# VectorE's reads of projections, bias products, norm roots and score tests issued one to three steps later

## Chip, core and metric

The kernel runs on one core of a Trainium2 chip, as one program. The metric is the device time of that core in microseconds (us), over all of its work from the inputs in HBM to the output in HBM. The core has five engines that run side by side, each in the order of its own queue: TensorE (PE; its weight loads are PEld), VectorE (DVE), ScalarE (ACT), GpSimd (POOL) and SyncE (SP), which here issues nearly all DMAs.

## What is computed

Four images of 32 x 32 positions with 256 channels pass through four layers. Layer 0 and the first part of layer 3 are state-space blocks with a scan over the 1024 positions; layer 1 is a grouped-convolution bottleneck; layer 2 is a masked attention and a mixture of eight experts; layer 3 ends with another mixture. Cut to what matters here, with the bookkeeping between the layers left out:

```python
# layer 0, one image; layer 3's scan is alike with 16 states instead of 64
x = conv3x3(layernorm(src) @ w_in)             # 512 channels, depthwise
x = gelu(x)
dt = softplus(dt_raw @ w_dt + dt_bias)          # dt_raw, Bm, Cm = split(x @ w_x)
def step(h, inp):
    xt, dtt, Bt, Ct = inp
    h = exp(dtt[:, :, None] * A) * h + (dtt * xt)[:, :, None] * Bt[:, None, :]
    return h, einsum('bdn,bn->bd', h, Ct)
out = src + layernorm(scan(step) + x * D_skip) @ w_out
# layer 1: relu(x + conv1x1(relu(conv3x3_grouped(relu(conv1x1(x))))))
# layer 2: y = layernorm(x + softmax(QK/sqrt(32) + mask) V Wo); then
#          y + sum over the best two of eight experts (gelu(y @ w1) @ w2)
# layer 3: scan block (gated by silu), then a second mixture of experts
```

## The kernel before, in words

**Scans.** The function `scans` (line 384) runs eight passes in the order of `SCANS` (line 32): (0,0), (0,1), (3,0), (0,2), (3,1), (0,3), (3,2), (3,3), where (0,b) is layer 0's scan of image b and (3,b) layer 3's. A pass of layer 0 has 256 units and one of layer 3 has 64, 1280 units together. A unit holds 128 pairs of channel and state on the partitions and all 1024 positions along the row. For each unit SyncE loads dt rows (dA), ScalarE makes the decay by an exponential, TensorE spreads the input of 32 channels over the partitions (`first`, tile ps_rep, bf16, two buffers of PSUM), VectorE multiplies by the B rows (TENSOR_TENSOR on ps_rep) and runs the scan instruction (TENSOR_TENSOR_SCAN, tile h), GpSimd multiplies h by the C rows, and for every two units TensorE collects the states (`pair`, tile ps_y). `scans` is a generator: it yields twice a unit, after the product and after the scan, so a unit has two half steps. Ahead of the last pass stand four empty units (`DRAIN`).

**Stages.** Everything else is written as twelve stages (`STAGES`, line 34), generators that yield after each small step: `front` makes layer 0's scan inputs of an image, `middle` takes the finished scan of layer 0 through `back0`, `layer1`, `attention`, `moe` and `front3`, which makes layer 3's scan inputs, and `last` takes layer 3's scan through `back3` and the second `moe` to the output. For image 3, `middle` is interleaved with `back3` and `moe` of image 2 (`beside`).

**What sets the order.** `run` (line 620) goes through the half steps of `scans` and after each draws up to two steps (`TICKS`) of the current stage by `advance`. It stops drawing in a half step when an engine's planned time has come ahead of VectorE's (`LEAD`), by fixed costs that the class `Metered` (line 99) adds up; these costs decide the order of instructions alone. `need` (line 583) is the one exception: when a pass is about to begin and its inputs are not yet made, it draws steps of the stage without any scan between them until they are. At the first pass, that is at the start, and at the last pass, (3,3), it has to.

**The reads.** `pipe` (line 200) runs a list of items through a list of functions, the second function one tick behind the first, the third two ticks behind, and yields once a tick. The usual first function is a product on TensorE into PSUM, and the second VectorE's read of it: in `back0` `turn` and `stats` (transposition and statistics), `project` and `add`; in `layer1` `up` and `add`; in `moe` `last` and `add` (the product of routing weights and biases, tile ps_b); in `back3` `project` and `add` (tile ps_o). `rstd` (line 254) computes 1/sqrt(v) for a normalisation: ScalarE takes Ln and Exp, then VectorE refines by one Newton step, four operations on `_w` and `_r` tiles straight behind; it is called by `norm` (tiles ln_, lnm_, lnt_, lny_) and by `back0` (b_). `large_scores` (line 1374) tests whether the scores of attention can grow large: squares on ScalarE, two products into ps_n, maxima on VectorE (top), a transposition by TensorE, and the comparison on VectorE (most, large), on which all engines then branch (line 1319). PSUM for the stages has three buffers that `ps` (line 194) hands out in turn.

Of the kernel before, what the change touches and what calls it, by code (L numbers as in the profile page):

```python
# [12 lines left out]
ALU = mybir.AluOpType  # L13
AX = mybir.AxisListType
# [6 lines left out]
TB = L // P  # L21
# [28 lines left out]
LEAD, LAG, TICKS = 0.0, 4.0, 2  # L50
# [89 lines left out]
END = object()  # L140


class Hybrid:
    def __init__(self, ctx, tc, a, out):
        self.ctx, self.tc, self.nc, self.a = ctx, tc, tc.nc, a
# [54 lines left out]
    def pipe(self, items, *steps, cost=1.0, cut=False):  # L200


        items = list(items)
        for tick in range(len(items) + len(steps) - 1):
            for s in reversed(range(len(steps))):
                if 0 <= tick - s < len(items):
                    steps[s](items[tick - s])
                    if cut and s:
                        yield cost
            yield cost if tick < len(items) else 0.5  # L210
# [43 lines left out]
    def rstd(self, pool, var, eps, n, tag):  # L254


        nc = self.nc
        v = pool.tile([P, n], F32, tag=tag + "_v", name=tag + "_v")
        nc.vector.tensor_scalar(v, var, eps, None, ALU.add)
        r = pool.tile([P, n], F32, tag=tag + "_r", name=tag + "_r")  # L260
        self.log_table()
        nc.scalar.activation(r, v, AF.Ln)
        nc.scalar.activation(r, r, AF.Exp, scale=-0.5)
        w = pool.tile([P, n], F32, tag=tag + "_w", name=tag + "_w")
        nc.vector.tensor_tensor(w, r, r, ALU.mult)
        nc.vector.tensor_tensor(w, w, v, ALU.mult)
        nc.vector.tensor_scalar(w, w, -0.5, 1.5, ALU.mult, ALU.add)
        nc.vector.tensor_tensor(r, r, w, ALU.mult)
        return r
# [4 lines left out]
    def norm(self, pool, src, n, out, tag):  # L274

        nc = self.nc
        mv = pool.tile([P, n, 2], F32, tag=tag + "_mv", name=tag + "_mv")

        def stats(j):
            st = pool.tile([P, 6], F32, tag=tag + "_st", name=tag + "_st", bufs=2)  # L280
            nc.vector.bn_stats(st, src[:, j, :])
            nc.vector.bn_aggr(mv[:, j, :], st)

        yield from self.pipe(range(n), stats, cost=0.8)
        r = self.rstd(pool, mv[:, :, 1], 1e-5, n, tag)
        yield 0.8
        b = pool.tile([P, n], F32, tag=tag + "_b", name=tag + "_b")
        nc.vector.scalar_tensor_tensor(b, mv[:, :, 0], -1.0, r, ALU.mult, ALU.mult)
        yield 0.5
        for j in range(n):  # L290
            nc.scalar.activation(
                out[:, j, :], src[:, j, :], AF.Identity, bias=b[:, j : j + 1], scale=r[:, j : j + 1]
            )
            if j % 4 == 3:
                yield 0.7
# [324 lines left out]
    def run(self):  # L620

        self.done, self.ready = set(), set()
        self.todo, self.stage, self.wait = list(STAGES), None, None
        self.alone, self.reached, self.passed = False, 0, set()
        nc, tc = self.nc, self.tc
        with tc.tile_pool(name="scan", bufs=1) as mp, tc.tile_pool(
            name="scps", bufs=1, space=PSUM
        ) as psum, tc.tile_pool(name="sdps", bufs=1, space=PSUM) as side, tc.manual_schedule():
            self.side_psum(side)
            self.scan_psum = psum  # L630
            self.mask_work, self.sorted = self.setup(), False
            clock = self.clock = dict.fromkeys(Metered.COST, 0.0)
            self.nc = Metered(nc, clock)
            for n, _ in enumerate(self.scans(mp, psum)):
                now = clock["vector"]
                if n % 2 and clock["gpsimd"] < now:
                    next(self.mask_work, None)
                for e in clock:
                    clock[e] = max(clock[e], now - LAG)
                for _ in range(TICKS):  # L640
                    if max(clock.values()) > clock["vector"] + LEAD or self.advance() is None:
                        break
            while self.advance() is not None:
                pass
            self.nc = nc
        assert not self.todo
# [275 lines left out]
    def back0(self, b, tb):  # L922


        nc, tc, vec = self.nc, self.tc, self.vec
        with tc.tile_pool(name=f"k{b}", bufs=1, side="right") as sp:
            nc.sync.dma_start(tb, self.image(self.a["x"].rearrange("b h w c -> (b h w) c"), b))
            y = sp.tile([P, DC, L], F32, name="y_back")
            u = sp.tile([P, DC, L], F32, name="u_back")
            w_out = sp.tile([P, DC, C], F32, name="w_out0")  # L930

            def fetch(d):
                nc.sync.dma_start(u[:, d, :], self.mem["u", 0, b, d])
                yield from self.scanned((0, b), [y[:, k, :] for k in range(DC)], d)

            def skip(d):
                nc.vector.scalar_tensor_tensor(
                    y[:, d, :], u[:, d, :], vec["L0_conv_D_skip"][:, d : d + 1], y[:, d, :],
                    ALU.mult, ALU.add,
                )  # L940

            yield 1.0
            yield from fetch(0)
            yield from self.add_rows(tb, self.bout0, TB)
            nc.sync.dma_start(w_out, self.mem[("w_out0",)])
            for d in range(1, DC):
                yield from fetch(d)
                for _ in range(4):
                    yield 0.5
                skip(d - 1)  # L950
                yield 1.3
            for _ in range(4):
                yield 0.5
            skip(DC - 1)
            yield 1.3
            mv = sp.tile([P, TB, 2], F32, name="b0mv")
            got = {}

            def turn(j):
                got[j] = ps = self.ps("ps_yt")  # L960
                for d in range(DC):
                    nc.tensor.transpose(
                        ps[:, d * P : (d + 1) * P], y[:, d, j * P : (j + 1) * P], self.ident
                    )

            def stats(j):
                st = sp.tile([P, 6], F32, tag="b0st", name="b0st", bufs=2)
                nc.vector.bn_stats(st, got.pop(j))
                nc.vector.bn_aggr(mv[:, j, :], st)

            yield from self.pipe(range(TB), turn, stats, cost=1.0)
            r = self.rstd(sp, mv[:, :, 1], 1e-5, TB, "b0")
            yield 0.8

            def project(j):
                got[j] = ps = self.ps("ps_o")
                for d in range(DC):
                    nc.tensor.matmul(
                        ps[:, :C], lhsT=y[:, d, j * P : (j + 1) * P], rhs=w_out[:, d, :],
                        start=(d == 0), stop=(d == DC - 1),  # L980
                    )

            def add(j):
                nc.vector.scalar_tensor_tensor(
                    tb[:, j, :], got.pop(j)[:, :C], r[:, j : j + 1], tb[:, j, :], ALU.mult, ALU.add
                )

            yield from self.pipe(range(TB), project, add, cost=1.7)

# [40 lines left out]
    def layer1(self, b, tb):  # L1032
        nc, tc = self.nc, self.tc
        with tc.tile_pool(name=f"l1{b}", bufs=1, side="right") as fp:
# [56 lines left out]
                nc.vector.tensor_tensor(tj, got.pop(j), tj, ALU.add)  # L1091
                nc.scalar.activation(tj, tj, AF.Relu)

            yield from self.pipe(range(TB // 2), up, add, cost=1.0)

# [276 lines left out]
    def large_scores(self, fp, qT, kT, large):  # L1374


        nc = self.nc
        sq = fp.tile([P, 2, 2, L], F32, name="sq")
        top = fp.tile([P, 2], F32, name="top2")
        for i, x in enumerate((qT, kT)):  # L1380
            for c in range(2):
                nc.scalar.activation(sq[:, i, c, :], x[:, c, :], AF.Square)
                yield 0.8
        for g in range(2):
            n2 = self.ps("ps_n2")
            for r in range(4):
# [2 lines left out]
                    rhs=sq[:, r // 2, r % 2, g * 512 : (g + 1) * 512],  # L1389
                    start=True, stop=True, tile_position=(0, 32 * r),  # L1390
                )
            nc.vector.tensor_reduce(top[:, g : g + 1], n2, AX.X, ALU.max)
            yield 1.3
        nc.vector.tensor_tensor(top[:, 0:1], top[:, 0:1], top[:, 1:2], ALU.max)
        ps = self.ps("ps_n3", (P, 2, 64))
        nc.tensor.transpose(ps[:1].rearrange("o i r -> o (i r)"), top[:, 0:1], self.ident)
        most = fp.tile([1, 2], F32, name="most")
        nc.vector.tensor_reduce(most, ps[:1], AX.X, ALU.max)
        nc.vector.tensor_tensor(most[:, 0:1], most[:, 0:1], most[:, 1:2], ALU.mult)
# [211 lines left out]
    def moe(self, which, b, tb, side="right", pause=False):  # L1611

        nc, tc, a = self.nc, self.tc, self.a
# [6 lines left out]
        with ExitStack() as stack:  # L1620
# [22 lines left out]
            with tc.tile_pool(name=f"mg{which}{b}", bufs=1, side=side) as gp:  # L1643
# [52 lines left out]
                    tj = tb[:, 2 * j : 2 * j + 2, :]  # L1696
                    nc.vector.tensor_tensor(tj, got.pop(j), tj, ALU.add)

                yield from self.pipe(range(TB // 2), last, add, cost=1.0)

            if pause:
                yield END
# [230 lines left out]
    def back3(self, b, tb, side="right", pause=False):  # L1933
        nc, tc = self.nc, self.tc
        with tc.tile_pool(name=f"h{b}", bufs=1, side=side) as sp:
# [68 lines left out]
                        add(j)  # L2004
                        yield 0.5
            else:
                yield from self.pipe(range(TB // 2), project, add, cost=3.4)

    def until(self, *what):
        while what not in self.passed:  # L2010
# [157 lines left out]
```

## Time and profile before

| | |
|---|---|
| median of 3 runs | 6303.35 us (6299.39 to 6311.23) |
| the profiled execution | 6294.21 us |
| its span, first to last instruction | 6292.5 us |
| mean granted TensorE clock | 0.842 |
| scan instruction (DVE, 128x1024) | 1280 times, 2285 ns, 2924.3 us |
| product ahead of it (DVE, ps_rep) | 1280 times, 1210 ns, 1549.4 us |
| product behind it (POOL, h) | 1280 times, 2366 ns, 3024.2 us |
| ACT, decay (two passes' kinds) | 1024 + 256 times, 1142 and 1143 ns |
| moved by DMA | 934.97 MB, 149 GB/s on the mean |

How to read it: times in a timeline are microseconds from the first instruction of the span. A row of groups has the line, the engine, the operation, the tiles out<-in, the shape and the count, then busy time and mean duration in ns, then idle time ahead of it and what ended that. Line 131 is the helper through which all recorded operations pass, so the tile's name tells the operation. A row of waits reads: engine and tile, what it waited for, microseconds in total, how often, and the longest. In rows by stretch, each engine's busy microseconds are followed by the number of its instructions; behind them stand the granted TensorE clock, the share of DMA engines busy, and GB/s.

### The profile page before, as it was taken

Reading aid. Unit: us, or ns where it says so; the run is one execution under the profiler, and the core shown is the slowest. Engines: PE = TensorE matmul, PEld = TensorE weight load, DVE = VectorE, ACT = ScalarE, POOL = GpSimd, SP = SyncE. Lnnn points to the kernel's source line nnn. Section 1 sums busy time; section 2 is a strip of 40 time slices with the busy share of each in tenths; the row PEclk is TensorE's granted clock in tenths of the full one; section 3 lists DMA queues with packets and bytes.
Section 4 is the critical chain, followed back from the end, with each engine's and each line's share of the span. In section 5 each row is a group of like instructions: output and inputs, shape, how many; then the busy total and the mean of one; then the engine's idle time right before and its main releaser. Section 6 shows DMA issues by size and latency. Waiting matters only on the chain. (4 is left out here: it accounts for less than half of the span.)

```text
span 6292.5 us, 59823 instructions
## 1 busy us (share of the span) xinstructions
PE 5142.7 (82%) x20249; PEld 2117.1 (34%) x20249; DVE 5032.7 (80%) x4016; ACT 3410.6 (54%) x4299; POOL 3825.9 (61%) x1948
## 2 busy tenths in 40 slices
PE   5676785579798568979869969989689779997999
PEld 2122120132253122234225522244145332543566
DVE  5888898988898998889889988899889982317811
ACT  3565655345496435558638735567547544336621
POOL 2787768665586766568767756577867752006600
PEclk7687785589798668979969979979779889999989
DMA  3555555544355656445455576345545761027611
GB/s 109 160 158 167 165 175 185 159 150 136 113 173 177 194 165 170 132 128 191 159 178 174 182 179 165 119 150 195 174 156 179 208 161 48 19 73 184 166 34 34
DMA packets 347915, 934.97 MB, mean 149 GB/s; under 512 B 37748, under 2 KB 120256, under 8 KB 345984
## 3 DMA queue, kind: packets, MB, share of 16 engines
q1 hardware_dynamic: 344880, 928.38, 48.7%
q0 software_dynamic: 2128, 2.13, 0.2%
q8 instruction: 165, 2.70, 0.2%
q14 instruction: 166, 1.36, 0.1%
q10 hardware_dynamic: 576, 0.39, 0.0%
HBM read 841.02 MB, written 92.37 MB: 148 GB/s over the span
## 5 line engine op out<-in xcount | busy, mean ns | idle before, releaser
L131 POOL TENSOR_TENSOR h<-h,rows 128x1024 f32<-128x1024 f32 x1280 | 3024.2, 2366 | 1740.4 <-DVE h L131 1529.3
L131 DVE TENSOR_TENSOR_SCAN h<-dA,ps_rep 128x1024 f32<-128x1024 f32 x1280 | 2924.3, 2285 | 182.2 <-ACT dA L131 53.6
L131 DVE TENSOR_TENSOR ps_rep<-ps_rep,rows 128x1024 f32<-128x1024 f32 x1280 | 1549.4, 1210 | 142.6 <-PE ps_rep L131 141.7
L131 PE MATMUL ps_rep<-S,spread_L_conv_A_log 96*128 96x512 bf16 x2048 | 752.8, 456 | 770.3 <-DVE h L131 722.4
L131 ACT ACTIVATE dA<-dA,A_L_conv_A_log 128x1024 f32<-128x1024 f32 x1024 | 1125.4, 1142 | 440.0 <-DMA dA<-dt 405.7
L131 PE MATMUL ps_y<-h,collect_L_conv_A_log 128*32 128x512 f32 x4096 | 704.4, 741 | 15.3 <-POOL h L131 15.3
L131 PE MATMUL ps_e<-we,h_m 128*128 128x256 f32 x3072 | 709.4, 383 | 8.3 <-ACT h_m L131 8.3
L131 PEld LDWEIGHTS <-spread_L_conv_A_log 96*128 96x128 bf16 x2048 | 159.7, 102 | 1558.0 <-DVE h L131 1246.4
L131 PEld LDWEIGHTS ps_e<-we,h_m 128*128 128x128 f32 x3072 | 583.3, 191 | 159.2 <-ACT h_m L131 31.0
L131 PE MATMUL ps_h<-xTm,we 128*128 128x512 f32 x1280 | 603.3, 607 | 4.6 <-DMA we<-in_L_ffn_W_dram 4.5
L131 ACT ACT_TABLE_LOAD x402 | 515.8, 1283 | 37.0 <-PE ps_h L131 15.5
L131 ACT ACTIVATE h_m<-ps_h,cols 128x512 f32<-128x512 f32 x384 | 257.5, 686 | 423.0 <-PE ps_h L131 421.0
L131 ACT ACTIVATE p<-ps_sc 128x512 f32<-128x512 f32 x404 | 219.3, 594 | 316.7 <-PE ps_sc L131 306.1
L131 ACT ACTIVATE dA<-dA,A_L_attn_A_log 128x1024 f32<-128x1024 f32 x256 | 282.8, 1143 | 141.4 <-DMA dA<-dt 122.8
L131 PEld LDWEIGHTS ps_h<-xTm,we 128*128 128x128 f32 x1280 | 242.2, 193 | 281.0 <-issue 211.5
L131 PE MATMUL ps_rep<-S,spread_L_attn_A_log 96*128 96x512 bf16 x512 | 176.8, 433 | 160.2 <-DVE h L131 138.6
L131 PE MATMUL ps_at<-p,v 128*32 128x512 f32 x1024 | 270.7, 608 | 0.2 <-ACT p L131 0.2
L131 PE MATMUL ps_at<-p,ones 128*32 128x512 f32 x1024 | 270.7, 608 | 0.0
L131 DVE SCALAR_TENSOR_TENSOR tb_rows<-ps_e,cw,tb_rows 128x256 f32<-128x256 f32 x128 | 55.7, 477 | 242.8 <-PE ps_e L131 242.7
L131 PE MATMUL ps_sc<-qT,kT 32*128 32x512 f32 x808 | 244.0, 654 | 4.6 <-ACT p L131 2.0
L131 PE MATMUL ps_cv<-pad,diag 128*128 128x512 f32 x504 | 230.5, 597 | 0.0
L131 PEld LDWEIGHTS ps_y<-h,collect_L_conv_A_log 128*32 128x32 f32 x4096 | 93.2, 118 | 339.7 <-issue 216.6
(347 smaller groups left out, 5475.6 us busy)
## 6 DMA issues: line engine op xcount, KB each, us to landing
dA<-dt SPq DMA_DIRECT2D x1280, 512.0 KB
we<-in_L_ffn_W_dram SPq DMA_DIRECT2D x64, 512.0 KB
parts<-parts SPq DMA_DIRECT2D x60, 384.0 KB
S<-parts SPq DMA_DIRECT2D x90, 256.0 KB
dt<-sp_r SPq DMA_DIRECT2D x64, 256.0 KB
y<-yo SPq DMA_DIRECT2D x128, 128.0 KB
y_back<-y SPq DMA_DIRECT2D x64, 256.0 KB
we<-in_L_ffn_w_dram SPq DMA_DIRECT2D x64, 256.0 KB
```

The costliest lines, as they stand in the source:

```text
L131: return got(*args, **kw)
```

## The change

A class `Slot` marks a yielded step that ends the half step's drawing: when `run` draws a `Slot`, it goes on to the next half step of the scans. `pipe` takes None as a function that does nothing, so that `pipe(items, product, None, read)` puts the read two ticks behind the product instead of one. This is done at five places (back0 twice, layer1, moe's bias product, back3 where it is not run beside another stage). `rstd` becomes a generator that yields three Slots between ScalarE's Exp and VectorE's refinement. `large_scores` issues both products, a Slot after each and one more, then both maxima, and another Slot behind the transposition. Nothing that is computed changes.

```diff
+class Slot(float):
+    pass
...
-                if 0 <= tick - s < len(items):
+                if steps[s] and 0 <= tick - s < len(items):
                     steps[s](items[tick - s])
...
         nc.scalar.activation(r, r, AF.Exp, scale=-0.5)
+        for _ in range(3):
+            yield Slot(0.5)
         w = pool.tile([P, n], F32, tag=tag + "_w", name=tag + "_w")
...
                 for _ in range(TICKS):
-                    if max(clock.values()) > clock["vector"] + LEAD or self.advance() is None:
+                    if max(clock.values()) > clock["vector"] + LEAD:
+                        break
+                    cost = self.advance()
+                    if cost is None or isinstance(cost, Slot):
                         break
...
-            yield from self.pipe(range(TB), turn, stats, cost=1.0)
-            r = self.rstd(sp, mv[:, :, 1], 1e-5, TB, "b0")
+            yield from self.pipe(range(TB), turn, None, stats, cost=1.0)
+            r = yield from self.rstd(sp, mv[:, :, 1], 1e-5, TB, "b0")
...
-            yield from self.pipe(range(TB), project, add, cost=1.7)
+            yield from self.pipe(range(TB), project, None, add, cost=1.7)
...
-            yield from self.pipe(range(TB // 2), up, add, cost=1.0)
+            yield from self.pipe(range(TB // 2), up, None, add, cost=1.0)
...
+        sums = []
         for g in range(2):
             n2 = self.ps("ps_n2")
...
-            nc.vector.tensor_reduce(top[:, g : g + 1], n2, AX.X, ALU.max)
-            yield 1.3
+            sums.append(n2)
+            yield Slot(1.3)
+        yield Slot(0.5)
+        for g in range(2):
+            nc.vector.tensor_reduce(top[:, g : g + 1], sums[g], AX.X, ALU.max)
         nc.vector.tensor_tensor(top[:, 0:1], top[:, 0:1], top[:, 1:2], ALU.max)
         ps = self.ps("ps_n3", (P, 2, 64))
         nc.tensor.transpose(ps[:1].rearrange("o i r -> o (i r)"), top[:, 0:1], self.ident)
+        yield Slot(0.5)
...
-                yield from self.pipe(range(TB // 2), last, add, cost=1.0)
+                yield from self.pipe(range(TB // 2), last, None, add, cost=1.0)
...
-                yield from self.pipe(range(TB // 2), project, add, cost=3.4)
+                yield from self.pipe(range(TB // 2), project, None, add, cost=3.4)
```

More of the change, by code (lines that the diff above doesn't have):

```diff
@@ L284, in norm @@
         yield from self.pipe(range(n), stats, cost=0.8)
-        r = self.rstd(pool, mv[:, :, 1], 1e-5, n, tag)
+        r = yield from self.rstd(pool, mv[:, :, 1], 1e-5, n, tag)
         yield 0.8
```

## Prediction

> **What bounds the kernel now.** I read the page's busy shares first, then VectorE's waits up to the last scan of the seventh pass, then the busy time by stretch, and last the two places that decide this change. VectorE is the busiest engine over most of the span:
>
> ```profile
> PE 5142.7 (82%) x20249; PEld 2117.1 (34%) x20249; DVE 5032.7 (80%) x4016; ACT 3410.6 (54%) x4299; POOL 3825.9 (61%) x1948
> ```
>
> Four stretches of busy time (PE, PEld, DVE, ACT, POOL, then the granted clock):
>
> ```profile
> 0.00:5230.10 5230.10, 4160.31 (x16443) 1579.30 (x16444) 4646.28 (x3467) 2989.55 (x3769) 3593.16 (x1819) 0.82 0.53 162
> 5230.10:5679.30 449.20, 418.33 (x1739) 194.54 (x1739) 90.30 (x233) 163.23 (x226) 37.27 (x29) 0.94 0.16 47
> 5679.30:5957.10 277.80, 250.14 (x958) 130.09 (x957) 244.44 (x184) 194.40 (x210) 188.11 (x95) 0.96 0.73 186
> 5957.10:6292.50 335.40, 313.93 (x1114) 213.17 (x1112) 51.63 (x133) 63.45 (x96) 7.31 (x5) 0.94 0.12 37
> ```
>
> The first is seven of the eight passes of scans (1216 of 1280), bound by VectorE at 89%. The second has no scan at all: the last pass needs what the stage of image 3 makes, the stage is not done, and TensorE works alone (93%). I call it the gap. The third is the last pass, the fourth the tail. VectorE's timeline shows the gap's two ends, and TensorE's (third line) where attention of image 3 ends:
>
> ```profile
> 5227.82 2.29 DVE L131 TENSOR_TENSOR_SCAN h<-dA,ps_rep 128x1024 f32<-128x1024 f32 x1 [0.39 <-ACT dA L131]
> 5679.32 1.23 DVE L131 TENSOR_TENSOR ps_rep<-ps_rep,rows 128x1024 f32<-128x1024 f32 x1 [4.55 <-PE ps_rep L131]
> 5396.85 3.29 PE L131 MATMUL ps_wo<-w_L_attn_Wo,raw 128*128 128x256 f32 x14 [1.93 <-POOL raw L131]
> ```
>
> So the time is the sum of the scans' stretch and the gap, then two stretches that the change hardly touches. VectorE's waits at the sites it moves, within the first stretch:
>
> ```profile
> DVE lny_w L131 <- ACT lny_r L131: 22.5, 6, 7.0
> DVE tb L131 <- PE ps_o L131: 21.2, 8, 6.0
> DVE tb L131 <- PE ps_b L131: 14.5, 7, 2.1
> DVE top L131 <- PE ps_n L131: 12.1, 8, 2.9
> ```
>
> With norm roots ln, lnm, b0, lnt (3.2+2.8+2.3+2.1), most (1.6) and b0's statistics (0.6) they make 82.9 us, the ceiling of the gain. 4.0 of it (top 3.0, most 0.5, lnt 0.5) belongs to image 3, and moves out of the stretch.
>
> **The reads that move: what each is worth.** No arithmetic is added; each read stands later in VectorE's queue.
>
> *Score test:* image by image, VectorE waits 3.0 us for two products (2.85 and 0.17), while TensorE is busy 28 us of the 40 from 1360. Two to three half steps lie between them now: all of 3 x 3.0 + 1.1 = 10 us goes.
>
> *Projection of the back part of pass type 3 (two images, 6.0 us each).* TensorE is in order and starts slow:
>
> ```profile
> 3219.20 0.69 DVE L131 TENSOR_TENSOR tb<-ps_o,tb 128x512 f32<-128x512 f32 x1 [5.97 <-PE ps_o L131]
> 3212.99 9.62 PE L131 MATMUL ps_o<-w_L_attn_W_out,y_back 128*128 128x256 f32 x32
> ```
>
> The next unit's broadcast (ps_rep) stands behind those 9.6 us. Without the read VectorE would do scan, product, scan and then wait for ps_rep from about 3219 to 3223: the wait changes its name and some 3 of 6 us are won, 2 x 3 = 6. Of b0's 9.8 us (9.2 of ps_o and 0.6 of statistics, pieces of some 2) I take 0.8: 8. Bias products, 14.5 us in pieces of 2: a lag of one tick can still fall into the same half step (two steps may be drawn per half step), so 0.6: 9. Sum with the score test: 33 us.
>
> *Norm roots.* 24 of them lie in the stretch (6 ln, 3 lnt, 6 lny, 5 lnm, 4 b0). Of their 32.4 us, three waits of 7.0 fall in the attention heads. There TensorE has no slack:
>
> ```profile
> 1480.00:1520.00 40.00, 39.88 (x232) 9.68 (x230) 35.65 (x21) 24.07 (x35) 24.07 (x11) 1.00 0.45 149
> 1520.00:1560.00 40.00, 39.66 (x219) 12.10 (x218) 35.92 (x24) 19.38 (x29) 22.53 (x10) 1.00 0.39 119
> 1560.00:1600.00 40.00, 37.70 (x216) 9.77 (x216) 31.70 (x31) 26.74 (x41) 24.35 (x12) 1.00 0.34 108
> ```
>
> In the 40 us with the 7.0 us wait TensorE idles only 2.3, at full clock; VectorE cannot run ahead of its ps_rep, so I credit 2.3 each: 7 us. Here a rule overstates: the Trainium skill (Perfetto Trace Analysis, Optimization Strategy) would have the gaps of the most-contended engine found and what blocks them made sooner; taken so, 3 x 7.0 = 21 us are won, and all moves together 79. The row says the most-contended engine is TensorE in that stretch. I use 7. The other 11.4 us of roots: 11, hence 18.
>
> Against it: the root's first operation multiplies two SBUF operands. Today it nearly always runs alone, because GpSimd has emptied its queue while VectorE does statistics and waits; three half steps later it stands straight between scan and product, where GpSimd is working. The row nearest to that is the split's subtraction, also of two SBUF operands in mid-scan:
>
> ```profile
> L131 DVE TENSOR_TENSOR sp_x<-sp_l,parts x64: 691/2002/2320, 108.4 to 5771.4; 128x512 f32<-128x512 f32 x64
> L131 DVE TENSOR_TENSOR lnm_w<-lnm_r x8: 166/168/168, 1685.5 to 6029.6; 128x8 f32<-128x8 f32 x8
> L131 DVE TENSOR_TENSOR lnt_w<-lnt_r x4: 167/1051/1940, 1328.7 to 5120.6; 128x8 f32<-128x8 f32 x4
> ```
>
> (min/median/max ns). One slow lnt_w, 5120.62 to 5122.56, ends just when a GpSimd product begun at 5120.19 does. The Trainium skill (SBUF — State Buffer, two separate sides) says why: such an operation and a GpSimd operation exclude each other, the later one waits out the whole instruction. By the rule's worst case 24 x 2.37 (GpSimd's h) = 57 us would be lost; by the row's mean (1.635 - 0.691 = 0.94) 24 x 0.94 = 23; none, if roots fall clear. I take 23. Roots together: 23 - 18 = 5 us lost.
>
> **What a Slot costs the stages.** A Slot ends the half step's turn, so other steps of the stage are not drawn: three half steps for each root, four for a score test. The stages thus lag behind the scans, and the order of the two programs shows it: the statistics ahead of attention (lnt_st) of images 0 to 3 stood after 277, 533, 862, 1190 scans, and stand after 279, 535, 876, 1216. The last is the end of the seventh pass. In before, image 3's ps_tr, ps_qk, ps_n, ps_v and 10 of 64 head steps were issued ahead of the gap, hidden by scans; in the changed program all of them follow the last scan. That is the new wait: the last pass, and everything after it, is queued behind them.
>
> *Gap, added.* From the last scan: layer 1's last adds, clearing mT, eight statistics (0.58 each) and the root, by the timeline's durations 8.6 us; image rows to turned (the same sequence at 5414.69 to 5420.97) 6.3; 32 ps_qk at 0.43 (27.47 us for 64 ps_c) plus 1.5 for a cold start, 15; last eviction 0.7 and four squares of 1.04, 5; ps_n 4; top and its turn 1.5; ps_v 8.5 (10.0 under scans, 7 at full clock); the branch on the test 1; fill 2. Sum 52. A head step takes 166.75 / 54 = 3.09 us (5230.10 to 5396.85; ps_sx counts 108, two a step), so ten more are 31. Total 83 us. Bounds: 70, if ps_v, squares and branch overlap; 95, if the mask's load is late. That DMA is passed by 13 others on SP now: four gates, eight y_back, w_out, 4.5 MB ahead of its 2 MB. At 5230 to 5260 DMA moved 167 GB/s, so it lands near 45 us, just ahead of the heads at 50: hidden, but with 5 us to spare.
>
> *Scans' stretch, relieved.* What leaves it: VectorE work of 13 us (those adds, statistics, root with its 1.94, test) and the ps_rep waits beside image 3's projections and heads, 4.83 + 4.57 + 1.35 = 11. Sum 24. The 4.0 us of waits leave too, and are in the 52.
>
> **Sum.** Stretch: -33 + 5 - 24 = -52. Gap: +83. Last pass and tail: 0, their steps after the last need number about the same. Net +31 us on 6294.21 (span 6292.5), hence 6325; the median of the runs, 6303.35, is 9 above that execution, and I give the prediction on the median: 6334.
>
> **Rivals.**
> *The reads give what their waits say (faster).* All 79 us go, roots meet no GpSimd instruction, and the gap grows by TensorE's work alone, 70. Then -79 - 24 + 70 = -33: 6270. It decides where VectorE's gain in the stretch exceeds the gap's growth. For it: every wait is real. Against: TensorE's full rows in the heads, and its queue at 3213. Chance 0.08.
> *A draw.* Lock and queue cost half of what I take, gap 75: about -70 + 75 = +5: 6308, chance 0.15.
> *Gains lost whole.* Roots at the worst case of the lock, reads again in the same half step, gap 95 with a late mask: 0 - 24 + 95 = +71: 6374. Chance 0.12.
> *Reads are not moved.* Excluded by the order: one to two scan operations more now stand between product and read, save at the last read of each pipe, which follows its neighbour.
> Forecast: 0.65.
>
> **Chances.** A difference of 0.2% (12.6 us) is about what a measurement of this kernel can tell. Slower 0.65 + 0.12 = 0.77, same 0.15, faster 0.08. Range: stretch -85 to -30, gap 70 to 95, ends not met together: -4 to +57, 6299 to 6360.
>
> **What will show it.** VectorE's last scan of the seventh pass should come near 5178, image 3's ps_qk after it, and the gap last about 532 us. Waits for ps_n, ps_o, ps_b and lny_r in the stretch should fall from 70 to under 25, those for ps_rep rise there outside image 3, and the first operation of the roots lengthen from 0.17 to about 1 us. It is wrong if the gap grows by under 60, if ps_rep waits fall as well, or if the last scan comes before 5150.

## The result, and the profile after

| | before | after |
|---|---|---|
| median | 6306.27 us (6 runs) | 6343.78 us (6 runs, 6333.77 to 6353.45) |
| the profiled execution, and its span | 6294.21, 6292.5 | 6344.47, 6342.7 |

The ratio is 1.0057, with a 95% interval of 1.0045 to 1.0070: slower by some 36 us. The four stretches of the changed kernel's busy time, cut at the same events as in before (PE, PEld, DVE, ACT, POOL, granted clock, DMA share, GB/s):

```profile
0.00:5207.31 5207.31, 4120.50 (x16152) 1544.95 (x16218) 4679.03 (x3435) 2957.97 (x3719) 3581.48 (x1811) 0.82 0.53 162
5207.31:5725.08 517.77, 469.68 (x1946) 215.26 (x1963) 103.77 (x266) 193.08 (x267) 47.09 (x37) 0.93 0.16 49
5725.08:6006.90 281.82, 254.72 (x958) 130.99 (x957) 244.12 (x184) 194.09 (x210) 187.66 (x95) 0.93 0.70 183
6006.90:6342.70 335.80, 313.95 (x1114) 213.23 (x1112) 51.53 (x134) 63.46 (x96) 7.29 (x5) 0.94 0.12 37
```

The stretch of scans is 22.8 us shorter (5230.1 to 5207.3), the gap 68.6 longer (449.2 to 517.8), the last pass 4.0 longer, the tail 0.4: together 50.2, the difference of the spans. The medians differ by 37.5 only; the profiled execution of before lies some 9 to 12 us below its medians. In the stretch VectorE works 33 us more (4646 to 4679), though the work of image 3 that left it was to take 13 away. The gap's beginning on TensorE, in the changed kernel's timeline:

```profile
5220.25 5.62 PE L131 MATMUL ps_tr<-ident,xa 128*128 128x128 f32 x16 [9.06 <-ACT xa L131]
...
5242.26 4.74 PE L131 MATMUL ps_n<-sq,byhead 128*32 128x512 f32 x16 [1.72 <-ACT sq L131]
...
5248.09 7.14 PE L131 MATMUL ps_v<-w_L_attn_Wv,xTa 128*128 128x256 f32 x32
5255.94 1.13 PE L131 MATMUL ps_sx<-qT,kT 32*128 32x512 f32 x4 [0.72 <-PEq L1425]
...
5445.35 4.97 PE L131 MATMUL ps_wo<-w_L_attn_Wo,raw 128*128 128x256 f32 x14 [1.93 <-POOL raw L131]
```

The last scan ends at 5207.31. Turning, projections, score test and ps_v of image 3 all follow it, and the first head step starts 48.6 us later. From there to the last ps_wo it is 189.4 us, where before had 166.75 left: 22.7. From ps_wo to the first product of the last pass: 279.7 against 282.5. Sum 48.6 + 22.7 - 2.7 = 68.6.

VectorE's waits in the stretch, first the largest one of before, then those of the changed kernel:

```profile
DVE ps_rep L131 <- PE ps_rep L131: 136.7, 102, 7.7
```
```profile
DVE ps_rep L131 <- PE ps_rep L131: 157.7, 114, 6.9
...
DVE y_back L131 <- DMA y_back<-y: 19.1, 5, 8.0
DVE tb L131 <- PE ps_b L131: 11.9, 12, 2.4
...
DVE tb L131 <- PE ps_o L131: 3.0, 6, 0.9
```

No line is left for lny_r or ps_n; ps_o fell from 21.2 to 3.0. The moved reads no longer wait (70.3 us in before, 14.9 now). But ps_rep waits rose by 21.0 in the stretch, and by 39.9 (117.1 to 157.0) up to unit 1152, where image 3's attention plays no part yet; those for y_back's loads rose by 10.3. Waits at reads that were not moved fell: sp_e and sp_x, behind ScalarE, by some 30 (96.7 to 67.2). Where VectorE's extra work comes from, in the changed kernel's timeline of VectorE and of GpSimd:

```profile
1598.46 2.29 DVE L131 TENSOR_TENSOR_SCAN h<-dA,ps_rep 128x1024 f32<-128x1024 f32 x1
1600.66 0.14 DVE L131 TENSOR_TENSOR lny_w<-lny_r 128x4 f32<-128x4 f32 x1
1600.83 0.17 DVE L131 TENSOR_TENSOR lny_w<-lny_w,lny_v 128x4 f32<-128x4 f32 x1
1601.03 2.23 DVE L131 TENSOR_SCALAR lny_w<-lny_w 128x4 f32<-128x4 f32 x1
1603.30 0.16 DVE L131 TENSOR_TENSOR lny_r<-lny_r,lny_w 128x4 f32<-128x4 f32 x1
```
```profile
1600.89 2.35 POOL L131 TENSOR_TENSOR h<-h,rows 128x1024 f32<-128x1024 f32 x1 [1.42 <-DVE lny_w L131]
```

GpSimd's product starts 0.23 us after the root does. The root's first two operations slip in before it, the third, 512 numbers, lasts 2.23 us and ends with the product (1603.26 and 1603.24). All 24 roots of the stretch are held: 17 in the third operation (2.21 to 2.27 us; all six ln, five of six lny, six of the other twelve), and seven in the first (1.15 to 1.50 us), which began while GpSimd was already at work and ended with its product. Beyond their usual 0.17 us these 24 operations take 44.0 us; in before, two roots were held, 3.5 us.

### The profile page after: what moved, and what is told of

It is laid out like the page before. It is cut to its first block, busy times and chain, and to the rows that moved or that the text cites. A ratio compares the mean times of both kernels' runs of the same rounds, so it can differ in the third digit from the quotient of the medians.

```text
span 6342.7 us, 59741 instructions
## 1 busy us (share of the span) xinstructions
PE 5158.8 (81%) x20166; PEld 2104.4 (33%) x20249; DVE 5078.5 (80%) x4016; ACT 3408.6 (54%) x4291; POOL 3823.5 (60%) x1948
## 5 line engine op out<-in xcount | busy, mean ns | idle before, releaser
L131 DVE TENSOR_TENSOR_SCAN h<-dA,ps_rep 128x1024 f32<-128x1024 f32 x1280 | 2924.2, 2284 | 182.8 <-ACT dA L131 49.5
L131 DVE TENSOR_TENSOR ps_rep<-ps_rep,rows 128x1024 f32<-128x1024 f32 x1280 | 1549.4, 1211 | 163.5 <-PE ps_rep L131 162.7
L131 PE MATMUL ps_y<-h,collect_L_conv_A_log 128*32 128x512 f32 x4096 | 719.0, 755 | 16.7 <-POOL h L131 16.7
L131 PE MATMUL ps_sc<-qT,kT 32*128 32x512 f32 x768 | 231.2, 653 | 5.8 <-DVE y_at L131 1.9
```

The lines of the kernel that those rows point to most:

```text
L131: return got(*args, **kw)
```

## Experiments

Theory at first: the lag of image 3 (how many scans its steps have fallen behind) sets the gap, and the moved reads win what the prediction said. Rival: what VectorE does not wait at a read, it waits at the next ps_rep. A third theory (where in the scans' half steps the attention heads fall) came from the first four runs. The results together (stretch, gap and ps_rep waits in us, from the profiled execution; "at" is the scan behind which image 3's lnt_st is issued; "heads" is attention's loop over heads, in images 0, 1, 2, from the end of VectorE's first `sums` operation to that of its last):

| kernel | median us | ratio (95%) | stretch | gap | at | ps_rep | heads |
|---|---|---|---|---|---|---|---|
| before | 6302.8 | 1 | 5230.1 | 449.2 | 1190 | 136.7 | 181.3, 181.3, 181.3 |
| changed | 6343.8 | 1.0057 (1.0045-1.0070) | 5207.3 | 517.8 | 1216 | 157.7 | 180.3, 180.3, 186.0* |
| no root Slots | 6336.5 | 1.0061 (1.0045-1.0078) | 5242.1 | 484.0 | 1198 | 168.9 | 195.0, 191.5, 195.1 |
| root Slots alone | 6359.7 | 1.0099 (1.0083-1.0114) | 5244.7 | 497.6 | 1207 | 165.7 | 180.6, 180.3, 186.0* |
| lag alone | 6378.3 | 1.0132 (1.0114-1.0149) | 5260.9 | 503.3 | 1211 | 174.3 | 189.7, 191.1, 187.7 |
| three steps | 6381.5 | 1.0138 (1.0120-1.0156) | 5313.4 | 444.7 | 1188 | 206.3 | 188.5, 188.5, 185.0 |
| two Slots | 6338.5 | 1.0057 (1.0038-1.0076) | 5253.7 | 463.8 | 1194 | 163.7 | 189.7, 191.9, 195.1 |
| four Slots | 6336.1 | 1.0051 (1.0034-1.0068) | 5252.4 | 477.2 | 1194 | 161.7 | 189.2, 181.3, 184.3 |
| score test alone | 6332.4 | 1.0045 (1.0031-1.0058) | 5250.1 | 464.2 | 1194 | 168.0 | 195.1, 193.9, 181.3 |
| score test, no Slots | 6289.3 | 0.9975 (0.9966-0.9984) | 5225.3 | 449.0 | 1190 | 147.3 | 181.3, 181.3, 181.3 |
| pipes alone | 6299.3 | 0.9988 (0.9975-1.0000) | 5197.1 | 481.8 | 1198 | 122.7 | 181.7, 181.3, 181.3 |
| no root Slots, shifted | 6295.3 | 0.9990 (0.9981-0.9999) | 5206.1 | 483.5 | 1202 | 153.1 | 181.7, 187.5, 184.3 |
| roots in three operations | 6340.8 | 1.0055 (1.0035-1.0074) | 5208.9 | 515.5 | 1216 | 164.5 | 180.3, 180.3, 182.8* |
| roots partly in PSUM | 6341.7 | 1.0054 (1.0034-1.0073) | 5218.5 | 516.4 | 1216 | 166.6 | 180.3, 180.3, 186.0* |

(* : these heads begin behind a product, and with root Slots they hold no wait of 7 us for lny's root, which all heads of the kernels without root Slots do. Stretch, gap, waits and heads are of one execution each, and executions of one kernel differ: 54 runs of before lay between 6285.3 and 6332.3 us. Each ratio is against the runs of before beside it, whose medians lay between 6298.6 and 6306.3. Last pass and tail lay between 276.6 and 281.8, and between 333.6 and 335.9, in all.)

**Without the roots' Slots.** `rstd` of the changed kernel:

```diff
-        for _ in range(3):
-            yield Slot(0.5)
+        yield from ()
```

> The changed kernel without the three Slots in the norm root; the lagged pipes and the score test stay. In its order the statistics ahead of image 3's attention stand after 1198 scans (before 1190, changed 1216). Lag theory (the gap grows 68.6 us over 26 units of lag, 2.6 each): gap +21 us to 470; stretch: moved reads of ps_n, ps_o, ps_b -34, ps_rep back +10, relief -8, so -32; net -11, 6295, ratio 0.998. Rival (moving those reads is what costs, by ps_rep waits): stretch not shorter than before, 6325 or more, ratio 1.003 or more.

The gap fell to 484, as the lag has it. But the stretch, with the operations no longer held, became 35 us longer than in the changed kernel, with ps_rep waits of 168.9. That fits the rival; the heads show later that it is something else.

**Root Slots alone.** The kernel before, with `rstd` as a generator with three Slots, and nothing else.

> The kernel before with the three Slots of the norm root alone; 1207 scans ahead of image 3's statistics. Lag theory: gap +45 us, relief of the stretch -16, roots themselves +5 (33 us of waits won, 38 us of longer root operations lost): +34, 6340, ratio 1.0054. Rival (lag is harmless, only the roots' own balance counts): +5, ratio 1.001.

Slower than the whole change. The waits for lny_r are gone, but VectorE's busy time in the stretch is 4693.0, 46.7 more than before, and ps_rep waits rose by 29. Up to unit 1152, ahead of image 3's attention, this kernel is 34.5 us behind before: ps_rep waits are 47.4 us up there and busy time 45.6, against 28.5 us of waits for the roots of lny, ln and lnm and 20.8 at sp_e and sp_x that went.

**Lag alone.** The kernel before, every read where it was; three Slots behind the finished root, and four around the score test:

```diff
         nc.vector.tensor_tensor(r, r, w, ALU.mult)
+        for _ in range(3):
+            yield Slot(0.5)
         return r
...
-            yield 1.3
+            yield Slot(1.3)
...
+        yield Slot(0.5)
+        yield Slot(0.5)
         yield 0.5
```

> The kernel before with every read where it was, and the same number of Slots put behind the reads (three behind the finished root, two in the score test's products, two behind its end); 1211 scans ahead of image 3's statistics. Lag theory: gap +55 us, relief -20: +35, 6341, ratio 1.0055. Rival (the reads' new places cost, not the lag): ratio 1.000. The root's third operation stays at 0.17 us in both.

The gap grew by 54, as expected of the lag. The stretch should have been shorter by the relief and is 31 us longer, with no root held (busy 4649.0): ps_rep +37.6, y_back's loads +13.7. A Slot costs in the stretch too, though it adds nothing there.

**Three steps in a half step** (`TICKS = 3` in the changed kernel), so that the stages catch up.

> The changed kernel with up to three steps drawn per half step instead of two (TICKS 3); all reads stay moved, and 1188 scans stand ahead of image 3's statistics, two fewer than before the change. Lag theory: gap 445, as before; stretch: reads of ps_n, ps_o, ps_b -34, roots +5, ps_rep +21 to +26: -5; net -8, ratio 0.9987. Rival (moved reads cost by themselves): gap short but the stretch longer than before by 20 or more, ratio 1.003 or more.

The gap is back at 444.7, and the stretch is 106 us longer than in the changed kernel, with ps_rep waits of 206.3. The work brought back among the scans is only a part of that: the stretch is also 83 us longer than in before, which has about the same work of image 3 ahead of the gap (1190 scans), with 70 us more of ps_rep waits and 45 of busy time. Three steps in a half step change the order of all stages, and this run cannot part the two.

**Two Slots, four Slots.** The kernel before with nothing but Slots behind the score test, two or four:

```diff
         nc.vector.tensor_copy(large, most[:, 0:1])
         yield 0.5
+        yield Slot(0.5)
+        yield Slot(0.5)
```

> The kernel before, with nothing but two Slots at the end of the score test: no read is moved, no root is split, but the heads of images 0 and 1 begin one unit later (unit 314 instead of 313), those of image 2 three units later, and image 3's attention statistics stand at scan 1194 instead of 1190. Theory (the heads have TensorE full, and what they cost depends on which half step of the scans each head step falls into): the 32 units from 320 and from 576, 136.5 us each in before, change by 8 us or more either way, with ps_rep waits changing alike, though nothing of their work has changed; gap 467, +18. If they go the way of the run without root Slots (150), the time is before +45, ratio 1.007; if not, +10. Rival (only the lag of image 3 matters): those units stay within 3 us, stretch -8, gap +18, ratio 1.0015.

> The kernel with two Slots behind the score test, with two more there (four in all): no read is moved, no root split. The heads of images 0, 1 and 2 begin at units 315, 571 and 901, each in the half step behind a scan, as in before (313, 569, 897), where with two Slots they began behind a product (314, 570, 900); image 3's statistics stand at scan 1194 in both. Theory (which half step the heads begin in decides): from the first to the last of the heads' sums 181 us in each image, as in before, where two Slots gave 189.7, 191.9 and 195.1; ps_rep waits there 5.3 instead of 12.8 to 18.6; stretch 33 us below two Slots, 5221; gap 464; ratio 1.001. Rival (delay of the heads by whole units is what costs): they stay above 188, ratio 1.0055.

Two Slots that move nothing else cost some 36 us, as much as the whole change: the heads, begun in the half step behind a product, take 189.7 to 195.1 us instead of 181.3. With four Slots all begin behind a scan, and image 1 is back at 181.3, image 2 near it, but image 0 took 189.2, and the total didn't move (the gap is 13 longer). Over the runs without root Slots and with two steps a half step, lag alone left aside, heads begun behind a product took 189.7 to 195.1 (eight), those begun behind a scan 181.3 to 189.2, 12 of 16 within 0.4 of 181.3. In lag alone, whose Slots also fall inside the heads, all three began behind a scan and took 187.7 to 191.1. So the half step matters, and isn't the whole of it.

The rest shows in TensorE's granted clock. The heads of image 0 in before, of image 0 with four Slots, and of image 2 with two:

```profile
1470.90:1652.20 181.30, 175.34 (x1014) 46.90 (x1006) 159.09 (x105) 107.68 (x157) 107.78 (x49) 1.00 0.39 125
```
```profile
1483.80:1673.00 189.20, 180.85 (x999) 48.68 (x1006) 159.47 (x105) 107.75 (x157) 107.89 (x49) 0.95 0.36 120
```
```profile
3921.40:4116.50 195.10, 183.24 (x998) 48.94 (x996) 158.98 (x104) 105.08 (x155) 107.80 (x49) 0.94 0.34 115
```

In all 14 traces, heads with a clock of 0.996 or more took 180.3 to 181.7 us, and the others, with 0.937 to 0.981, took 182.8 to 195.1. What is lost is about the clock's share: 0.981 of 184.3 us is 3.5 us lost, and these heads are 3.0 longer; 0.938 of 195.1 is 12.1 lost, and 13.8 longer. The clock falls to a half behind an idle time of TensorE, where ps_rep waits for VectorE to finish lny's root. In before and with four Slots, image 0:

```profile
1580.25 0.60 PE L131 MATMUL ps_rep<-S,spread_L_conv_A_log 96*128 96x512 bf16 x2 [2.01 <-DVE lny_b L131]
```
```profile
1594.87 0.60 PE L131 MATMUL ps_rep<-S,spread_L_conv_A_log 96*128 96x512 bf16 x2 [2.01 <-DVE lny_b L131]
```

The idle time is the same, and the clock stayed at 1.00 in before, but fell at 1595.7 for 13.7 us with four Slots. Behind a product this idle time is 4.6 us, and the clock fell each time (eight of eight). Behind a scan it is 2.0 to 2.3 us. In the records the clock changes only on a grid of 3.41 us; in four of the 16 heads the idle time lies whole within one step of the grid, in 12 a grid point divides it, and the clock fell in those four and in none of the 12. The grid lies at another offset from the span's start in each trace (0.7 to 3.4 us), so which heads are long is in part chance of the execution. This is read from the traces; no run was made to test it, and it is not a whole rule: idle times of 0.97 us, which heads behind a product have too, mostly made the clock fall as well.

**Score test alone, with and without Slots.** The changed `large_scores` in the kernel before; in the second, a Slot doesn't end the half step:

```diff
-                    if cost is None or isinstance(cost, Slot):
+                    if cost is None:
```

> The kernel before with the score test of the changed kernel alone (both products, then both maxima, Slots between); roots and pipes as before. The heads of images 0 and 1 begin at unit 314 as in the kernel with two Slots, image 3's statistics at scan 1194 as there. VectorE's 12.1 us of waits for ps_n and 1.6 for the transposition go to under 1. Theory (what VectorE does not wait at ps_n it waits at the next ps_rep, TensorE being behind): within 5 us of the kernel with two Slots in the stretch. Rival (the waits are won whole): the stretch is 9 to 10 us shorter than with two Slots, ratio 0.0015 below it.

> The kernel before with the score test of the changed kernel (both products, then both maxima, then the transposition, and its maximum a step later), but its Slots drawn as plain steps, so that no half step's drawing ends for it: nothing else is changed. Heads begin at 313, 569 and 897 as in before, image 3's statistics stand at scan 1190 as in before; so neither lag nor half step differs. VectorE's waits at top and most, 12.1 and 1.6 us, go. Theory A (a read's wait is won where TensorE is not behind): stretch 8 to 12 us shorter, gap 449, ratio 0.9983. Theory B (it comes back at the next ps_rep): ps_rep waits rise by 8 or more, ratio 0.9995 to 1.0005.

With Slots, the stretch is 3.6 us below that of two Slots: no wait for ps_n is left there, where two Slots had 10.1 at top, and ps_rep has 4.3 more. That is within what theory expected. Without Slots, one can see the place where the wait goes, at the start of image 0's heads. VectorE and TensorE in before:

```profile
1404.24 2.29 DVE L131 TENSOR_TENSOR_SCAN h<-dA,ps_rep 128x1024 f32<-128x1024 f32 x1
1409.67 1.23 DVE L131 TENSOR_TENSOR ps_rep<-ps_rep,rows 128x1024 f32<-128x1024 f32 x1 [3.15 <-PE ps_rep L131]
```
```profile
1403.28 2.56 PE L131 MATMUL ps_sc<-qT,kT 32*128 32x512 f32 x4 [0.26 <-ACT p L131]
...
1409.02 0.61 PE L131 MATMUL ps_rep<-S,spread_L_conv_A_log 96*128 96x512 bf16 x2
```

and VectorE in the kernel with the score test alone and no Slots:

```profile
1401.78 2.29 DVE L131 TENSOR_TENSOR_SCAN h<-dA,ps_rep 128x1024 f32<-128x1024 f32 x1
1409.84 1.23 DVE L131 TENSOR_TENSOR ps_rep<-ps_rep,rows 128x1024 f32<-128x1024 f32 x1 [5.77 <-PE ps_rep L131]
```

VectorE comes 2.5 us earlier, and waits 2.6 longer: ten units on, TensorE does the first heads at half clock (2.56 us for four ps_sc, against 1.13 later), and ps_rep stands behind them. The same 20.5 us in before, and in the kernel with the score test alone and no Slots:

```profile
1394.60:1415.10 20.50, 18.07 (x71) 4.77 (x72) 14.94 (x9) 4.51 (x8) 16.05 (x9) 0.75 0.38 121
```
```profile
1394.60:1415.10 20.50, 18.72 (x54) 4.48 (x58) 12.61 (x7) 3.26 (x6) 14.47 (x8) 0.50 0.34 107
```

The clock was full again at 1409.1 in before, at 1415.1 here: a quarter of 20.5 us, 5.1, is lost. At the test the kernel had gained 5.1 us (units 285 to 295), and here it loses them (295 to 300). In images 1 and 2 it gains 5.1 and 4.0 and loses 4.9 and 3.0, with 10.2 and 6.7 us more at half clock. At image 3 the clock rose 7.6 us earlier than in before, and the gain stays. So in these two traces the wait comes back where TensorE's clock rises later.

In the stretch 9.7 + 1.6 us of waits went from top and most, and 10.6 came to ps_rep: theory B. The time does not follow that reading: it is 13.5 us below before's (6289.33 against 6302.83), theory A's size. The two profiled spans differ by 6.8, with 8.3 us won in the last 32 units ahead of the gap, where image 3's score test stands; before's profiled execution lies 8.6 below its median, this one's 2.0, so the traces show half of the difference and leave the rest open. This kernel is faster than the two with Slots at this place (6332.4 and 6338.5).

**Pipes alone.** The kernel before, with None in the five pipes.

> The kernel before with only the five pipes of the changed kernel (reads two ticks behind); roots and score test as in before, no Slot at all. Heads begin at 313, 569 and 901, behind a scan; image 3's statistics at scan 1198 instead of 1190. VectorE's waits for ps_o (21.2) should fall below 4 and for ps_b from 14.5 to 9. Gap by the lag: 476 to 484, +27 to +35. Theory B (half comes back as ps_rep waits, and the lag brings some relief): stretch -20, ratio 1.002. Theory A (won whole, 24, and 10 of relief): stretch -34, ratio 1.000.

VectorE's waits in the stretch:

```profile
DVE ps_rep L131 <- PE ps_rep L131: 122.7, 103, 7.5
...
DVE tb L131 <- PE ps_b L131: 8.9, 10, 1.0
```

No line for ps_o, and at unit 1152 ps_rep waits are 115.9 us against 117.1 in before: nothing came back. (In the whole stretch they are 14 less, nearly all of it in the last 64 units, where image 3's work has left.) At unit 1152 it is 26.1 us ahead of before, and 25.1 us of waits for ps_o and ps_b have gone: these reads are won whole. At the stretch's end it is 33.1 ahead. The lag of eight scans (gap +32.6) takes it back: within 0.12% of before.

**Without root Slots, shifted.** The first experiment with one Slot more at the end of the score test.

> The changed kernel without the roots' Slots, with one Slot more at the end of the score test: all other reads are moved as in the changed kernel. Heads begin at 315, 571 and 905, behind a scan (without this Slot at 314, 570, 902, behind a product); image 3's statistics at scan 1202 instead of 1198. Theory (half step): the heads take 181 to 182 us each instead of 195.0, 191.5 and 195.1, so the stretch is 38 us below the kernel without root Slots, 5204, the gap about 486; ratio 1.001, from 1.0061: with more Slots it is faster. Rival (the moved reads' waits come back as ps_rep waits wherever they fall): heads stay at 190 or more, ratio 1.006.

With one more Slot, and a later image 3, it is 41 us faster than the first experiment, and not slower than before. Its heads took 181.7, 187.5 and 184.3, where 181 to 182 was expected. So that experiment's long stretch was mostly where the heads fell: of the 36.0 us by which the stretch shrank, 28.1 are in the three heads' times as listed. From here to the changed kernel it is the roots' Slots, less the one just added: 1.2 us in the stretch, 34.3 in the gap, 4.1 in the last pass, 6295.3 against 6343.8 us. They are the loss: the gap for the most part, by the lag that they add. That is 40.2 of 48.5 us; this kernel's profiled execution lies 9.0 above its median, so some 8 us are not placed.

**Roots in three operations, roots partly in PSUM.** The changed kernel, with the refinement in other forms:

```diff
-        nc.vector.tensor_tensor(w, w, v, ALU.mult)
-        nc.vector.tensor_scalar(w, w, -0.5, 1.5, ALU.mult, ALU.add)
-        nc.vector.tensor_tensor(r, r, w, ALU.mult)
+        nc.vector.scalar_tensor_tensor(w, w, -0.5, v, ALU.mult, ALU.mult)
+        nc.vector.scalar_tensor_tensor(r, w, 1.5, r, ALU.add, ALU.mult)
```
```diff
-        w = pool.tile([P, n], F32, tag=tag + "_w", name=tag + "_w")
+        if tag in ("ln0", "lny", "lnm"):
+            w = pool.tile([P, n], F32, tag=tag + "_w", name=tag + "_w")
+        else:
+            w = self.ps("ps_" + tag, (P, n))
```

> The changed kernel with the root's refinement in three operations of VectorE instead of four: r*r, then (w*-0.5)*v, then (w+1.5)*r, so the TENSOR_SCALAR, which took 2.2 us in 20 of 24 roots of the stretch, is gone. Theory (timing: GpSimd's product begins some 0.3 us behind the scan, and whichever operation on two SBUF operands comes at that point is held for its length): the second or third operation now lengthens to about 2.2, VectorE's busy time in the stretch stays within 10 us of the changed kernel's 4679.6, time within 0.15% of the changed kernel, ratio 1.0055. Rival (the form TENSOR_SCALAR is what collides): all root operations stay under 0.3 us, busy 33 us less, time 20 to 30 us below the changed kernel, ratio 1.0015.

> The changed kernel with the refinement's w in PSUM for the roots ln, b0 and lnt (14 of 24), so that their last three operations have an operand in PSUM; lny and lnm keep SBUF, as a control in the same run. Theory (the exclusion is between VectorE and GpSimd over SBUF operands only): the third operation of ln, b0 and lnt falls from 2.2 to under 0.3 us, that of lny and lnm stays at 2.2; busy 20 to 25 us less than 4679.6. If VectorE's time is what those places cost, the stretch is 20 us shorter and the ratio about 1.0025; if TensorE has them (ps_rep), the ps_rep waits rise by most of it and the time stays within 10 us of the changed kernel. Rival (the long operations are not an exclusion over SBUF): no operation shortens.

Groups of the stretch (count, busy us, mean ns), in the kernel with three operations, then in that with PSUM:

```profile
L131 DVE SCALAR_TENSOR_TENSOR ln_r<-ln_w,ln_r 128x8 f32<-128x8 f32 x6 | 13.5, 2242 | 0.2
```
```profile
L131 DVE SCALAR_TENSOR_TENSOR ln_b<-ln_mv,ln_r 128x8 f32<-128x8 f32 x6 | 10.9, 1814 | 0.2
...
L131 DVE TENSOR_SCALAR ps_ln<-ps_ln 128x8 f32<-128x8 f32 x6 | 1.0, 174 | 0.2
```

In three operations, the third is held again, as a SCALAR_TENSOR_TENSOR: it is not the form TENSOR_SCALAR alone. In PSUM the TENSOR_SCALAR falls from 2247 to 174 ns, while lny's stays at 1888; but ln_b, the next operation on SBUF operands alone, 168 ns elsewhere, now takes 1814. The first operation, which squares an SBUF tile into PSUM, was held as before where it came late (1.48 to 1.50 us, four times). Busy time fell by 7.5 us instead of 20 to 25, and the time did not move.

## Why the prediction came out as it did

Forecast +31 (6334), measured +37.5 on the medians and +50.2 between the profiled executions: slower, by the mechanism that was named: the gap grew by more than the stretch won. The sizes inside were off, and that the total came near is in part luck.

*Gap, +83: right in kind, 68.6 in size.* In the table the gap goes with the lag from 444.7 us at 1188 scans to 517.8 at 1216, 2.6 us a scan. The 52 us to the first head were 48.6. The ten head steps at 3.09 = 31 were 22.7: in before TensorE still worked until 5234.51, 4.4 us behind the last scan, on head steps that had been issued ahead of it, so those weren't hidden whole; the other 4 us stay open. The mask's load was not late.

*Moved reads, -33: right for the pipes, wrong for the score test.* The pipes' terms (6 + 8 + 9 = 23) are 26.1 us at unit 1152 in the kernel with pipes alone. The score test's 10 come back, by the traces, as 10.6 of ps_rep waits; the prediction had TensorE busy 28 of 40 us at the test and did not look ten units on, nor at when the clock rises there.

*Roots, +5: the step that failed.* The held operations cost 44.0 us, not 23, and VectorE's busy time rose by 46.7 with root Slots alone. The prediction took the mean of the sp_x row, 0.94 a root, and named the first operation. In 17 of 24 it was the third, and a hit is not a mean: 2.08 us (2.25 less 0.17). The gain of 18 did not come either: all 33 us of root waits went, but with root Slots alone ps_rep waits rose by 47.4 up to unit 1152. The worst case by the rule of the Trainium skill (SBUF — State Buffer, two separate sides), the whole of GpSimd's 2.37 us, was nearer than the row. And the three head waits credited with 2.3 each gave nothing in images 0 and 1: without lny's waits (7.5 us an image) the heads took 33.3 us beyond the 3.5 of scan and product a unit, 32.6 before (42 and 42.5 units), ps_rep waits being 9.7 instead of 5.3. Up to unit 1152 root Slots alone cost 34.5; with the pipes' -26.1 that makes +8.4, and the changed kernel is +7.0 there, where the prediction had -28.

*Relief, -24:* the last 64 units took 29.8 us less; ps_rep waits there fell by 18.9 (19.6 to 0.7), where the prediction had 11. So the stretch gave -22.8 (7.0 - 29.8), not -52, and the last scan came at 5205, not 5178.

*Signs.* Waits for ps_n, ps_o, ps_b and lny_r fell from 70 to 15 and ps_rep waits rose, as said. The total is near because two errors partly cancel, the stretch 29 too short and the gap 14 too long, and because the medians differ by less than the two profiled executions. The roots' first operation was to lengthen to about 1 us; it did in seven, to 1.15 to 1.50, and in 17 the third did. "Reads give what their waits say" failed at the roots. What the prediction did not hold as a case at all is the half step in which the heads begin and the clock that TensorE then has, worth 8 to 14 us an image behind a product; in the changed kernel images 0 and 1 happened to fall well, with the clock at 1.00, and image 2 did not (186.0, at 0.96).

## What to carry to other kernels

A wait on the bounding engine is a gain only if the next thing it needs is not as late: follow the engine on to its next wait for the same producer before crediting it. When work is interleaved by a generator, whatever ends a turn delays the whole later program, so price the delay where the last stage is exposed (here 2.6 us a scan) beside the wait that is saved; a move that ends no turn, like the score test without Slots, kept its gain. And compare variants only at the same alignment: an empty step can cost as much as the change under study. Where the same work takes longer in one variant, look at the granted clock of that stretch before the order of instructions is blamed.

## What the runs showed of the hardware

- TENSOR_TENSOR, TENSOR_SCALAR and SCALAR_TENSOR_TENSOR of the norm roots, on SBUF operands alone, issued while GpSimd's 2.37 us product ran, lasted until that ended: 0.17 us became up to 2.25. Statistics on SBUF tiles were not held: all 140 BATCH_NORM operations of the changed kernel that began at least 0.1 us inside a product and 0.8 us ahead of its end were done before it (0.40 and 0.18 us on the mean).
- With an input in PSUM such an operation took 0.17 us in the same place, and the hold passed to the next one without (ln_b, 0.17 to 1.81); in two roots of b0 the next was VectorE's product on ps_rep, and nothing was held. An output in PSUM alone did not help: 1.48 to 1.50 us.
- Which of several quick operations is hit depends on when GpSimd starts (0.23 us behind the root's first: the third; ahead of the root: the first), for TENSOR_SCALAR and SCALAR_TENSOR_TENSOR alike.
- The same head matmuls took 2.56 us for four at a granted clock of 0.50, as the heads began, and 1.13 at 1.00 a few us later.
- An idle time of TensorE of 2.0 to 2.3 us in the heads halved the granted clock when it lay within one step of the 3.41 us grid of the clock's records (four of four), and did not when a grid point divided it (none of 12); 4.6 us did each time (eight of eight).
